# Four graph layers in one kernel: moves between partitions taken from DMA to TensorE, layer 1 nested, tables issued by ScalarE, other buffers and plan constants

## The chip, the cores and the metric

One core of a Trainium2 chip runs the whole program. The metric is the device time of one execution in microseconds (us); the time before is the median of nine runs. The engines are named as in the profile: PE (matmul), PEld (its weight loads), DVE (VectorE), ACT (ScalarE), POOL (GpSimd), SP (SyncE, which here only issues DMAs).

## The reference

Sixteen graphs of 1024 nodes with 64 features each pass four layers. `adj` is a 0/1 matrix with about four neighbours per node. Each layer normalizes its input, applies relu and adds its result to `x`:

```python
# layer 0: one normalized hop (adjacency plus self), one weight, relu
h = relu(layernorm(x)); x = x + relu(norm_adj @ (h @ L0_kernel))
# layer 1: h and its three hops side by side, one weight over all four
g = (adj + I) * d[:, None] * d[None, :]          # d = 1 / (sqrt(row sum) + 1e-7)
outs = [h, g @ h, g @ g @ h, g @ g @ g @ h]
x = x + concat(outs) @ L1_W.T + L1_b
# layer 2: for each node, sort its neighbours' features (self included, some removed
# when there are more than ten), weighted sum of three quantiles, then a small MLP
agg = 0.25*q(0.25) + 0.5*q(0.5) + 0.25*q(0.75)
x = x + (relu((h + agg) @ W1 + b1) @ W2 + b2) * nodemask
# layer 3: one plain hop
x = x + adj @ (h @ L3_weight) + L3_bias
```

## The kernel before

**Per graph.** `fast` runs over the graphs `b`; `first(b)` notes the stages graph, rank, lists, table and layer1, and `second(b)` the stages sort and out. All instructions are first noted by a planner and later issued.

- graph (`fast_graph`): eight row tiles of 128x1024 are loaded by SP into five `row` buffers. ACT counts neighbours (`junk_row`), PE transposes the row, ACT copies it into `at` (fp8), DVE finds up to eight neighbours per node (`found`).
- rank (`by_degree`): nodes are sorted by their number of neighbours, so that the sort later needs few slots for most; `near` holds the neighbour numbers in that order.
- lists (`dilated`): removals, weights, and the indices for the gathers: `idx`, `self_idx` and `shared_idx`.
- table and layer1 (`fast_to_table`): layers 0 and 1. A hop is `fast_product`: `u` is split into three bf16 parts, and each part gives 16 matmuls against `at`; `add_turned` adds the self term, and ACT copies the sum out (`prod_sb`, features on partitions). The normalized result `h2` is then written to a table in DRAM, from which POOL gathers.
- sort (`fast_quantiles`): POOL gathers neighbours' rows from the table into the slots of `a`, DVE sorts the slots (`a` and `b` by turns), weighs and sums them.
- out (`unsorted`, `fast_to_output`): one-hot matrices `back` bring the result to node order, then the MLP and layer 3.

**Shared gathers.** Slot `k` of node tile `s` is full (128 rows) or only partly used. The partial slots, 13 pieces (`packed`), are packed into four gathers of up to 128 rows (`staged0` to `staged3`). A piece that begins at row `at` of its gather must begin at row 0 in `a`. So each piece is moved twice between partitions: its indices into `shared_idx` (line 1274, in the lists stage), and its gathered rows out of `staged` into `a` (line 1373, in the sort stage). Both are SBUF-to-SBUF DMAs issued by SP, 26 per graph. The unused rows of `a` are filled with a large number by ACT (`a<-big`).

**Layer 1.** After `h`, DVE makes `u` for the first hop. Aside from that PE transposes `h`, multiplies it with the first weight block, and the result with the bias is added to `x`. Each of three hops gives `prod_sb`, which goes through its weight block into the PSUM bank `acc` (`times`), and in the first two hops also through a transpose into the next `u`. The sum in `acc` is scaled and added to `x`.

**Order.** `Plan` decides the order of every engine's instructions ahead of time. `cost` gives each instruction a length and a landing time (a plain DMA: 0.1 us of its issuing queue). `order` gives each step a wanted time from its chain within the graph, `PERIOD` per graph and an offset `LATER` per stage, lists the steps engine by engine (`listed`), repeats that `PASSES` times and keeps the list with the shortest length by its own costs. On the chip each engine and SP take their lists strictly in order. Buffers, which the planner knows, limit how many graphs are under way: four `at`, five `x`, two `near`. PSUM's banks are named per phase by `bank`.

Of the kernel before, what the change touches and what calls it, by code (L numbers as in the profile page):

```python
# [11 lines left out]
F32 = mybir.dt.float32  # L12
# [4 lines left out]
U32 = mybir.dt.uint32  # L17
AF = mybir.ActivationFunctionType
ALU = mybir.AluOpType
# [22 lines left out]
    "_0": dict(u=1, prod_sb=1),  # L42
    "_1": dict(u=2, h=1, h2=2, prod_sb=2, ft_sb=1),
    "_b": dict(agg=1, ft_sb=1, hid=1, u=1, prod_sb=1),
}
ROW_BUFS = 5
PASSES = 3
PERIOD = 474.0

LATER = dict(  # L50
    graph=-2909.0, rank=-1697.0, lists=-2440.0, table=-1118.0, layer1=688.0, sort=610.0, out=2073.0
)
# [41 lines left out]
def over_features(v):  # L94

    return v.unsqueeze(2).to_broadcast([v.shape[0], v.shape[1], F])
# [265 lines left out]
def cost(engine, op, out, ins, kw):  # L362
# [8 lines left out]
    if op == "dma_start":  # L371
        return 0.1, 2.2 if n < N else 3.6
    if engine == "tensor":
# [35 lines left out]
class Kernel:  # L409
# [7 lines left out]
    def constants(self, pool, work, psum):  # L417
# [60 lines left out]
        self.bias_parts = {}  # L478
        for name in ("L1_gnn_b", "L2_gnn_b2", "L3_gnn_bias"):
# [42 lines left out]
    def sorted_constants(self, pool, work, psum):  # L522
# [30 lines left out]
        self.before = pool.tile([w, w], BF16, name="before")  # L553
        nc.vector.tensor_scalar(self.before, kv[0:w, :], kvt, None, ALU.is_lt)

        node = self.counted(work, work, "node_of", [HT, 2], [[P, HT], [HT * P, 2]], step=1)
# [471 lines left out]
    def fast_pools(self, ctx):  # L1028
        def pool(what, bufs, space=None):
            made = self.pool(ctx, f"fast_{what}", bufs, space)  # L1030
            return Phased(self, PlanPool(self.plan, made, bufs, space is PSUM))

        self.plan = Plan(self.nc)
        self.p_at = pool("at", 4)
        self.p_small = pool("small", 2)
# [45 lines left out]
    def by_degree(self, b, n1, found):  # L1081
# [71 lines left out]

        near = self.p_lists.tile([P, T + 1, E], F32, name="near")
        nc.scalar.copy(near[:, 0, :], ps[:, 0, 0:E])
# [5 lines left out]
    def dilated(self, b, near, meta):  # L1161
# [107 lines left out]
        nc.vector.tensor_copy(idx, near)  # L1269
        shared = packed()  # L1270
        shared_idx = self.p_lists.tile([P, len(shared)], U32, name="shared_idx")
        for g, group in enumerate(shared):
            for s, k, at, r in group:
# [32 lines left out]
        nc.vector.tensor_tensor(flat, flat, part[:, 2], ALU.add)  # L1306
        return idx, shared_idx, self_idx, weights

# [14 lines left out]
    def fast_quantiles(self, table, lists):  # L1323

        nc = self.nc
        idx, shared_idx, self_idx, weights = lists
        agg = self.activations("agg")
        shared = packed()
        staged = []
        for g, group in enumerate(shared):  # L1330
            t = self.p_lists.tile([P, F], F32, name=f"staged{g}", bufs=1)
            r = sum(x[3] for x in group)
            self.gather(t[0:r, :], table, shared_idx[0:r, g : g + 1])
            staged.append(t)
        for lo, hi, n, halves in WIDTHS:

            alone = halves > 0
            count = hi - lo + halves - alone
            a = self.p_sort.tile([P, count * n * F], F32, name=f"a{n}", bufs=2)
            b = self.p_sort.tile([P, count * n * F], F32, name=f"b{n}", bufs=1)  # L1340
            av = a.rearrange("p (g k f) -> p g k f", g=count, f=F)

            def place(s, k):
                return (k // n, k % n) if s == 0 else (s - lo + halves - alone, k)

            for s in range(lo, hi):
                rows = rows_of(s)
                cap = len(rows)

                empty = [k for k, r in enumerate(rows) if r < P]  # L1350
                empty += range(cap + 1, n * (2 if halves and s == 0 else 1))
                while empty:
                    group, k = place(s, empty[0])
                    many = 1
                    while many < len(empty) and place(s, empty[many]) == (group, k + many):
                        many += 1
                    nc.scalar.copy(
                        av[:, group, k : k + many, :],
                        self.big.unsqueeze(1).to_broadcast([P, many, F]),
                    )  # L1360
                    empty = empty[many:]
                own = self.own(idx, s)
                group, k = place(s, cap)
                self.gather(av[:, group, k, :], table, self_idx[:, s : s + 1])
                for k, r in enumerate(rows):
                    if r == P:
                        group, i = place(s, k)
                        self.gather(av[:, group, i, :], table, own[:, k : k + 1])
            for t, members in zip(staged, shared):
                for s, k, at, r in members:  # L1370
                    if lo <= s < hi:
                        group, i = place(s, k)
                        nc.sync.dma_start(out=av[0:r, group, i, :], in_=t[at : at + r, :])
            r = self.sorted_slots(a, n, F, b)
# [41 lines left out]

    def fast_product(self, at, u, plus_self):

        nc = self.nc
        ps = self.bank("prod", (P, HT * P))  # L1420
        for n, part in enumerate(self.parts(u)):
# [223 lines left out]
    def fast_to_table(self, b, at, rs, table):  # L1645

        nc = self.nc
        x = self.p_x.tile([P, T, F], F32, name="x", bufs=5)
        for half in range(2):
# [22 lines left out]
        self.times(ps, pt, 0)  # L1672
        y = self.p_x.tile([P, T, F], F32, name="y", bufs=1)
        self.by_node(y, ps, AF.Relu, d0)
# [4 lines left out]
        self.phase, self.plan.stage = "_1", "layer1"  # L1679
        norm, = self.fast_normed(0, x, None)  # L1680
        h = self.activations("h")
        self.by_node(h, x, AF.Relu, *norm)
        u = self.factor("u")
        nc.vector.tensor_tensor(u, h, over_features(d1), ALU.mult)
        ps = self.bank("node", (P, HT * P))
        for q in range(HT):
            pair = h[:, 2 * q : 2 * q + 2, :].rearrange("p h f -> p (h f)")
            nc.tensor.transpose(ps[:, q * P : (q + 1) * P], pair, self.ident)
        ht = self.factor("ft_sb").rearrange("p s f -> p (s f)")
        nc.scalar.copy(ht, ps)  # L1690
        ps = self.bank("node")
        self.biased(ps, "L1_gnn_b")
        self.times(ps, ht, 1, start=False, one_group=True)
        nc.vector.tensor_tensor(x, x, ps, ALU.add)
        acc = self.bank("acc")
        for k in range(1, 4):
            pt = self.fast_product(at, u, True)
            self.times(acc, pt, 1 + k, start=k == 1, stop=k == 3, one_group=True)
            if k < 3:
                ps = self.bank("node")  # L1700
                for q in range(HT):
                    nc.tensor.transpose(
                        ps[:, 2 * q : 2 * q + 2, :], pt[:, q * P : (q + 1) * P], self.ident
                    )
                u = self.factor("u")
                self.by_node(u, ps, AF.Copy, d11)
        y = self.p_x.tile([P, T, F], F32, name="y", bufs=1)
        self.by_node(y, acc, AF.Copy, d1)
        nc.vector.tensor_tensor(x, x, y, ALU.add)
# [5 lines left out]
        for half in range(2):  # L1715
            nc.sync.dma_start(
                out=nodes(table[0:N, :].rearrange("(o n) f -> o n f", o=1), half),
                in_=h[:, half::2, :],
            )
        return x, h  # L1720

    def fast_to_output(self, b, at, x, ot):
# [4 lines left out]
        for half in range(2):  # L1727
# [4 lines left out]
            for q in range(HT):  # L1732
# [6 lines left out]
                )  # L1739
        y = self.p_x.tile([P, T, F], F32, name="y", bufs=1)  # L1740
        mask = self.mask[:, b * T : (b + 1) * T]
# [99 lines left out]
```

## Time and profile before

| | |
|---|---|
| nine runs | 1745.21 to 1766.52 us, median 1755.19 us |
| profiled execution | 1746.21 us |
| its span, first to last instruction | 1744.3 us |
| granted TensorE clock, mean | 0.798 |
| busy: DVE, PE, POOL, ACT | 1150.4, 1113.9, 964.1, 838.9 us |
| HBM read and written | 103.05 MB and 8.39 MB |

The profiled execution is one run; durations of instructions come from it. Busy times count an engine's own work; time in which it waits for a semaphore or only issues a DMA is not busy. All instructions of the planner carry the line of its issuing loop (L351), so they are told apart by what they write and read: `a<-staged` is the move of gathered rows into `a`, `shared_idx<-idx` that of the indices, `table<-h` the write of a table. An fp32 matmul stands in the trace as two records. The chain of work that ended last is followed back from the last instruction; `SPq` in it is time in which SP's queue issued DMAs, and "another core or an unknown queue" is waiting whose releaser the profile can't name.

### The profile page before, as it was taken

The page shows a single profiled execution, that of the slowest core. Times are in us where ns is not written, and L with a number is a line of the kernel's source. Part 1 is how long each engine was busy: PE and PEld are TensorE (multiplying, and loading weights), DVE is VectorE, ACT ScalarE, POOL GpSimd, SP SyncE. Part 2 cuts the span into 40 slices and gives each one's busy share as a digit, 9 for nine tenths or more (in the row PEclk, how much of TensorE's full clock was granted, in tenths as well). Part 3 has the DMA queues.
Part 4 walks back from the last instruction along what each step waited for, and adds up shares of the span by engine and source line. Part 5 has one row for each costly group of instructions (what it writes and reads, how often), then busy time and mean ns, then how long its engine had stood idle before and what let it go on. Part 6 is the DMA issues. An engine that isn't in the chain of part 4 may idle for free.

```text
span 1744.3 us, 24520 instructions
## 1 busy us (share of the span) xinstructions
PE 1113.9 (64%) x7784; PEld 625.9 (36%) x7784; DVE 1150.4 (66%) x2929; ACT 838.9 (48%) x2307; POOL 964.1 (55%) x767
## 2 busy tenths in 40 slices
PE   2664496778586675867478685847468665583345
PEld 1342253344253342434244353423234342341122
DVE  6953275588786684948478695847668476676381
ACT  4864352475555472645266565535365453433021
POOL 0006327487668284736728484855838467586700
PEclk9886697788888896888689797968779678696657
DMA  5433101132313141221323222221213121111100
GB/s 162 144 109 98 51 16 47 33 105 64 107 46 103 38 123 53 56 75 48 104 52 105 58 79 68 91 53 44 79 47 108 44 65 33 25 33 31 29 8 9
DMA packets 117624, 115.20 MB, mean 66 GB/s; under 512 B 87692, under 2 KB 88044, under 8 KB 117484
## 3 DMA queue, kind: packets, MB, share of 16 engines
q1 hardware_dynamic: 91756, 82.08, 15.5%
q0 software_dynamic: 25344, 31.38, 8.0%
q8 instruction: 64, 1.05, 0.2%
q14 instruction: 76, 0.62, 0.1%
q10 hardware_dynamic: 384, 0.07, 0.0%
HBM read 103.05 MB, written 8.39 MB: 64 GB/s over the span
## 4 chain that ended last, share of the span: by engine, by line
DVE 28%; issue 17%; another core or an unknown queue 15%; PE 13%; ACT 9%; SPq 7%; DMA 6%; POOL 4%; DVEq 0%; POOLq 0%; ACTq 0%
PE prod L351 10%; DVE b L351 7%; SPq L351 7%; DVE a L351 5%; POOL a L351 4%; DVE found L351 3%; DMA row<-in_adj_dram 2%; PE node L351 2%; ACT junk_row L351 1%; DVE stats L351 1%; ACT u L351 1%; DVE x L351 1%; DVE rest L351 1%; ACT y L351 1%
## 5 line engine op out<-in xcount | busy, mean ns | idle before, releaser
L351 POOL DMA_INDIRECT a<-table,idx x512 | 661.4, 1292 | 162.0 <-issue 155.3
L351 POOL DMA_INDIRECT a<-table,self_idx x128 | 166.9, 1304 | 236.1 <-DMA table<-h 76.7
L351 PE MATMUL prod<-at,u 128*64 128x512 fp8e4 x1280 | 207.9, 446 | 68.9 <-ACT u L351 36.5
L351 DVE TENSOR_TENSOR b<-a 128x768 f32<-128x768 f32 (+4 forms) x224 | 177.8, 824 | 88.6 <-DMA a<-staged 65.1
L351 PE MATMUL prod<-at,rest 128*64 128x512 fp8e4 x1280 | 188.1, 421 | 33.1 <-DVE rest L351 16.8
L351 DVE TENSOR_TENSOR a<-b 128x1536 f32<-128x1536 f32 (+4 forms) x192 | 199.1, 1070 | 4.4 <-ACT b L351 3.3
L351 PE MATMUL prod<-at,lo 128*64 128x512 fp8e4 x1280 | 177.1, 396 | 30.6 <-issue 25.6
L351 ACT CAST at<-tr 128x1024 fp8e4<-128x1024 bf16 x128 | 127.6, 1022 | 142.2 <-remote 107.0
L351 ACT ACTIVATE junk_row<-row,unit 128x1024 bf16<-128x1024 f32 x128 | 148.0, 1156 | 67.6 <-DMA row<-in_adj_dram 65.8
L351 DVE TENSOR_SCALAR back<-numbers,meta 128x1024 bf16<-128x1024 f16 x128 | 61.3, 488 | 157.4 <-remote 91.7
L351 DVE FIND_INDEX8 found<-ones,row 128x8 uint32<-128x1032 f32 x128 | 156.4, 1225 | 0.0
L351 POOL DMA_INDIRECT staged<-table,shared_idx x64 | 81.4, 1272 | 131.1 <-DMA table<-h 62.0
L351 PE MATMUL tr<-ident_bf,row 128*128 128x128 bf16 x1024 | 90.5, 235 | 97.1 <-ACT at L351 68.4
L351 PEld LDWEIGHTS <-u 128*64 128x64 bf16 x1280 | 77.5, 123 | 186.5 <-issue 70.4
L351 PEld LDWEIGHTS <-lo 128*64 128x64 bf16 x1536 | 94.6, 115 | 137.6 <-issue 63.2
L351 PEld LDWEIGHTS <-rest 128*64 128x64 bf16 x1536 | 93.4, 120 | 132.6 <-issue 50.4
L351 ACT COPY prod_sb<-prod 128x512 f32<-128x512 f32 x80 | 46.9, 587 | 171.8 <-PE prod L351 120.1
L351 ACT ACTIVATE h<-x,norm_bias,rstd 128x64 f32<-128x64 f32 x256 | 90.1, 434 | 60.7 <-DVE norm_bias L351 46.5
L351 PEld LDWEIGHTS <-row 128*128 128x128 bf16 x1024 | 70.9, 106 | 122.8 <-issue 118.0
L351 PE MATMUL prod<-back,agg 128*64 128x512 bf16 x256 | 66.6, 458 | 70.0 <-DVE back L351 30.0
L351 PE MATMUL prod<-ident,u 128*128 128x128 f32 x512 | 87.3, 311 | 24.5 <-issue 24.3
L351 ACT COPY b<-a 128x768 f32<-128x768 f32 (+2 forms) x128 | 69.0, 588 | 60.0 <-DVE a L351 46.9
(209 smaller groups left out, 1983.3 us busy)
## 6 DMA issues: line engine op xcount, KB each, us to landing
row<-in_adj_dram SPq DMA_DIRECT2D x128, 512.0 KB
a<-table,idx POOLq DMA_INDIRECT x512
x<-in_x_dram SPq DMA_DIRECT2D x32, 128.0 KB
table<-h SPq DMA_DIRECT2D x32, 128.0 KB
out_dram<-x SPq DMA_DIRECT2D x32, 128.0 KB
a<-table,self_idx POOLq DMA_INDIRECT x128
staged<-table,shared_idx POOLq DMA_INDIRECT x64
a<-staged SPq DMA_DIRECT2D x32, 20.0 KB
```

The source lines that it names most:

```text
L351: f(*[real(x) for x in s.args], **{k: real(x) for k, x in s.kw.items()})
```

## The change

- The two moves of each piece become matmuls with a shifted matrix of ones (`shift`, built once). The index move reads `near` (fp32) instead of `idx` and is made in the sort stage; its 13 one-column products of a graph go to the PSUM bank `moved`, and ACT copies them to `shared_idx`. Each piece of `staged` is a product of 64 columns into `moved` (eight pieces to a bank), which ACT copies into `a`. The fills of `a` come first for all slots.
- Layer 1 is written as a nested sum: the last block's product first, then for each of three hops `d11` times the sum, a hop, and the next block added inside `fast_product` by one 512-column product (`more`). The bank `acc` is gone; each hop ends in four transposes. `h` of layer 1 is not made, `u` is made at once with the root of the degree in its factor, and the bias is added on DVE.
- The tables are written from ACT's queue instead of SP's.
- `y` uses `u`'s buffers; `at` has five buffers, `x` six, `near` three, `ft_sb` of layer 1 two.
- `cost` gives a plain DMA 0.35 or 0.5 us instead of 0.1; `PERIOD` and `LATER` have other values.

```diff
-    "_1": dict(u=2, h=1, h2=2, prod_sb=2, ft_sb=1),
+    "_1": dict(u=2, h2=2, prod_sb=2, ft_sb=2),
...
-PERIOD = 474.0
+PERIOD = 566.0
-    graph=-2909.0, rank=-1697.0, lists=-2440.0, table=-1118.0, layer1=688.0, sort=610.0, out=2073.0
+    graph=-1558.0, rank=-1340.0, lists=-1357.0, table=-796.0, layer1=-156.0, sort=321.0, out=1580.0
...
     if op == "dma_start":
-        return 0.1, 2.2 if n < N else 3.6
+        return 0.35 if n == N else 0.5, 2.2 if n < N else 3.6
...
+        d = self.counted(work, work, "col_past", [3 * P], [[1, 3 * P]], base=-P, step=-1)
+        self.shift = pool.tile([P, 3 * P], F32, name="shift")
+        nc.vector.tensor_scalar(self.shift, d, 0.0, None, ALU.is_equal)
...
-        self.p_at = pool("at", 4)
+        self.p_at = pool("at", 5)
...
-        near = self.p_lists.tile([P, T + 1, E], F32, name="near")
+        near = self.p_lists.tile([P, T + 1, E], F32, name="near", bufs=3)
...
-                nc.sync.dma_start(
-                    out=shared_idx[at : at + r, g : g + 1], in_=self.own(idx, s)[0:r, k : k + 1]
-                )
...
+        ps = self.bank("moved")
+        for g, group in enumerate(shared):
+            for n, (s, k, at, r) in enumerate(group):
+                nc.tensor.matmul(
+                    ps[:, 0, g : g + 1],
+                    lhsT=self.shift[0:r, P - at : 2 * P - at],
+                    rhs=self.own(near, s)[0:r, k : k + 1],
+                    start=n == 0,
+                    stop=n == len(group) - 1,
+                )
+        shared_idx = self.p_lists.tile([P, len(shared)], U32, name="shared_idx")
+        nc.scalar.copy(shared_idx, ps[:, 0, 0 : len(shared)])
+        pieces = [(g, *x) for g, group in enumerate(shared) for x in group]
+        staged = {}
+        for first in range(0, len(pieces), T):
+            ps = self.bank("moved")
+            some = pieces[first : first + T]
+            for n, (g, s, k, at, r) in enumerate(some):
+                rows = sum(x[3] for x in shared[g])
+                if g not in staged:
+                    staged[g] = self.p_lists.tile([P, F], F32, name=f"staged{g}", bufs=1)
+                    self.gather(staged[g][0:rows, :], table, shared_idx[0:rows, g : g + 1])
+                nc.tensor.matmul(
+                    ps[0:r, n, :],
+                    lhsT=self.shift[0:rows, P + at : P + at + r],
+                    rhs=staged[g][0:rows, :],
+                    start=True,
+                    stop=True,
+                )
+            for n, (g, s, k, at, r) in enumerate(some):
+                av, group, i = places[s, k]
+                nc.scalar.copy(av[0:r, group, i, :], ps[0:r, n, :])
...
-            for t, members in zip(staged, shared):
-                for s, k, at, r in members:
-                    if lo <= s < hi:
-                        group, i = place(s, k)
-                        nc.sync.dma_start(out=av[0:r, group, i, :], in_=t[at : at + r, :])
...
+            if more and n == 0:
+                nc.tensor.matmul(ps, lhsT=more[0], rhs=more[1], start=False, stop=False)
...
-        x = self.p_x.tile([P, T, F], F32, name="x", bufs=5)
+        x = self.p_x.tile([P, T, F], F32, name="x", bufs=6)
...
-        norm, = self.fast_normed(0, x, None)
-        h = self.activations("h")
-        self.by_node(h, x, AF.Relu, *norm)
+        norm, = self.fast_normed(0, x, root)
         u = self.factor("u")
-        nc.vector.tensor_tensor(u, h, over_features(d1), ALU.mult)
+        self.by_node(u, x, AF.Relu, *norm)
...
         ps = self.bank("node")
-        self.biased(ps, "L1_gnn_b")
-        self.times(ps, ht, 1, start=False, one_group=True)
-        nc.vector.tensor_tensor(x, x, ps, ALU.add)
-        acc = self.bank("acc")
-        for k in range(1, 4):
-            pt = self.fast_product(at, u, True)
-            self.times(acc, pt, 1 + k, start=k == 1, stop=k == 3, one_group=True)
...
+        self.times(ps, gt, 4)
+        for k in range(3, 0, -1):
+            u = self.factor("u")
+            self.by_node(u, ps, AF.Copy, d11)
+            pt = self.fast_product(at, u, True, (self.wbd[:, k, :], gt))
+            ps = self.bank("node")
+            for q in range(HT):
+                nc.tensor.transpose(
+                    ps[:, 2 * q : 2 * q + 2, :], pt[:, q * P : (q + 1) * P], self.ident
+                )
+        y = self.factor("u")
+        self.by_node(y, ps, AF.Copy, d1)
+        nc.vector.tensor_tensor(x, x, over_tiles(self.bias["L1_gnn_b"]), ALU.add)
         nc.vector.tensor_tensor(x, x, y, ALU.add)
...
-            nc.sync.dma_start(
+            nc.scalar.dma_start(
                 out=nodes(table[0:N, :].rearrange("(o n) f -> o n f", o=1), half),
```

More of the change, by code (lines that the diff above doesn't have):

```diff
@@ L478, in constants @@
         self.bias_parts = {}
-        for name in ("L1_gnn_b", "L2_gnn_b2", "L3_gnn_bias"):
+        for name in ("L2_gnn_b2", "L3_gnn_bias"):
             rest = work.tile([1, F], F32, name="bias_rest")
@@ L1269, in dilated @@
         nc.vector.tensor_copy(idx, near)
[L1270 to L1273, printed above, removed]
-                nc.sync.dma_start(
-                    out=shared_idx[at : at + r, g : g + 1], in_=self.own(idx, s)[0:r, k : k + 1]
-                )
         self_idx = self.p_lists.tile([P, T], U32, name="self_idx")
@@ L1306, in dilated @@
         nc.vector.tensor_tensor(flat, flat, part[:, 2], ALU.add)
-        return idx, shared_idx, self_idx, weights
+        return idx, near, self_idx, weights
     def own(self, idx, s):
@@ L1325, in fast_quantiles @@
         nc = self.nc
-        idx, shared_idx, self_idx, weights = lists
+        idx, near, self_idx, weights = lists
         agg = self.activations("agg")
         shared = packed()
[L1329 to L1334, printed above, removed]
+        sorts, places = [], {}
         for lo, hi, n, halves in WIDTHS:
@@ L1339, in fast_quantiles @@
             a = self.p_sort.tile([P, count * n * F], F32, name=f"a{n}", bufs=2)
+            sorts.append((lo, hi, n, halves, alone, count, a))
+            av = a.rearrange("p (g k f) -> p g k f", g=count, f=F)
+            for s in range(lo, hi):
+                for k in range(n * (halves if halves and s == 0 else 1)):
+                    group = k // n if s == 0 else s - lo + halves - alone
+                    places[s, k] = av, group, k % n
+        for s in range(T):
+            rows = rows_of(s)
+            empty = [k for k, r in enumerate(rows) if r < P]
+            empty += [k for q, k in places if q == s and k > len(rows)]
+            while empty:
+                av, group, k = places[s, empty[0]]
+                many = 1
+                while many < len(empty) and places[s, empty[many]][1:] == (group, k + many):
+                    many += 1
+                nc.scalar.copy(
+                    av[:, group, k : k + many, :],
+                    self.big.unsqueeze(1).to_broadcast([P, many, F]),
+                )
+                empty = empty[many:]
@@ L1340, in fast_quantiles @@
+        for lo, hi, n, halves, alone, count, a in sorts:
             b = self.p_sort.tile([P, count * n * F], F32, name=f"b{n}", bufs=1)
-            av = a.rearrange("p (g k f) -> p g k f", g=count, f=F)
-            def place(s, k):
-                return (k // n, k % n) if s == 0 else (s - lo + halves - alone, k)
             for s in range(lo, hi):
                 rows = rows_of(s)
[L1348 to L1364, printed above, removed]
@@ L1365, in fast_quantiles @@
+                av, group, i = places[s, len(rows)]
+                self.gather(av[:, group, i, :], table, self_idx[:, s : s + 1])
                 for k, r in enumerate(rows):
                     if r == P:
-                        group, i = place(s, k)
-                        self.gather(av[:, group, i, :], table, own[:, k : k + 1])
-            for t, members in zip(staged, shared):
-                for s, k, at, r in members:
-                    if lo <= s < hi:
-                        group, i = place(s, k)
-                        nc.sync.dma_start(out=av[0:r, group, i, :], in_=t[at : at + r, :])
+                        av, group, i = places[s, k]
+                        self.gather(av[:, group, i, :], table, self.own(idx, s)[:, k : k + 1])
@@ L1415, in parts, with fast_product @@
         yield lo
-    def fast_product(self, at, u, plus_self):
+    def fast_product(self, at, u, plus_self, more=None):
         nc = self.nc
@@ L1672, in fast_to_table @@
         self.times(ps, pt, 0)
-        y = self.p_x.tile([P, T, F], F32, name="y", bufs=1)
+        y = self.factor("u")
         self.by_node(y, ps, AF.Relu, d0)
@@ L1679, in fast_to_table @@
         self.phase, self.plan.stage = "_1", "layer1"
-        norm, = self.fast_normed(0, x, None)
-        h = self.activations("h")
-        self.by_node(h, x, AF.Relu, *norm)
+        norm, = self.fast_normed(0, x, root)
         u = self.factor("u")
-        nc.vector.tensor_tensor(u, h, over_features(d1), ALU.mult)
+        self.by_node(u, x, AF.Relu, *norm)
         ps = self.bank("node", (P, HT * P))
         for q in range(HT):
-            pair = h[:, 2 * q : 2 * q + 2, :].rearrange("p h f -> p (h f)")
+            pair = u[:, 2 * q : 2 * q + 2, :].rearrange("p h f -> p (h f)")
             nc.tensor.transpose(ps[:, q * P : (q + 1) * P], pair, self.ident)
-        ht = self.factor("ft_sb").rearrange("p s f -> p (s f)")
-        nc.scalar.copy(ht, ps)
+        gt = self.factor("ft_sb").rearrange("p s f -> p (s f)")
+        nc.scalar.copy(gt, ps)
         ps = self.bank("node")
-        self.biased(ps, "L1_gnn_b")
-        self.times(ps, ht, 1, start=False, one_group=True)
-        nc.vector.tensor_tensor(x, x, ps, ALU.add)
-        acc = self.bank("acc")
-        for k in range(1, 4):
-            pt = self.fast_product(at, u, True)
-            self.times(acc, pt, 1 + k, start=k == 1, stop=k == 3, one_group=True)
[L1699 to L1708, printed above, removed]
+        self.times(ps, gt, 4)
[7 more added lines that the diff above has]
+                    ps[:, 2 * q : 2 * q + 2, :], pt[:, q * P : (q + 1) * P], self.ident
+                )
+        y = self.factor("u")
+        self.by_node(y, ps, AF.Copy, d1)
+        nc.vector.tensor_tensor(x, x, over_tiles(self.bias["L1_gnn_b"]), ALU.add)
         nc.vector.tensor_tensor(x, x, y, ALU.add)
@@ L1739, in fast_to_output @@
                 )
-        y = self.p_x.tile([P, T, F], F32, name="y", bufs=1)
+        y = self.factor("u")
         mask = self.mask[:, b * T : (b + 1) * T]
```

## The prediction

> **What bounds the kernel now.** I read the busy row and the chain first, then the waits, then one stretch of the timeline.
>
> The page's busy row and chain rows:
>
> ```profile
> PE 1113.9 (64%) x7784; PEld 625.9 (36%) x7784; DVE 1150.4 (66%) x2929; ACT 838.9 (48%) x2307; POOL 964.1 (55%) x767
> ...
> DVE 28%; issue 17%; another core or an unknown queue 15%; PE 13%; ACT 9%; SPq 7%; DMA 6%; POOL 4%; DVEq 0%; POOLq 0%; ACTq 0%
> ```
>
> No engine is full. Per graph (a sixteenth) DVE does 71.9 us, PE 69.6, ACT 52.4, POOL 60.3. POOL's share is too low: the waits below show 624 gaps of about 0.3 us between gathers, so the gathers hold POOL for some (964.1 + 190.2)/16 = 72 us. The first and last table writes are issued at 134.7 and 1579.0 us, so a graph takes (1579.0 - 134.7)/15 = 96.3 us. Some 20 to 25 us per graph are thus waiting that no engine's load explains, and 7% of the chain, 122 us, is SP doing nothing but issue DMAs.
>
> The whole program's waits:
>
> ```profile
> POOL a L351 <- issue: 190.2, 624, 0.5
> POOL a L351 <- DMA table<-h: 76.7, 3, 32.4
> DVE b L351 <- DMA a<-staged: 65.1, 8, 13.5
> POOL staged L351 <- DMA table<-h: 62.0, 2, 49.7
> POOL staged L351 <- DMA a<-staged: 52.0, 6, 21.0
> ```
>
> POOL waits for tables, DVE's sort for the moved pieces, and the next graph's shared gathers for the same moves. All are transfers of SP's queue. The timeline around 780 us shows how they hang together (start, length, engine, in brackets the idle time before):
>
> ```profile
> 770.50 9.74 SPq L351 DMA_DIRECT2D shared_idx<-idx  x13
> ...
> 780.42 8.14 SPq L351 DMA_DIRECT2D a<-staged  x11
> 788.67 0.93 SPq L351 DMA_DIRECT2D table<-h  x2
> 789.70 0.97 SPq L351 DMA_DIRECT2D row<-in_adj_dram  x2
> 790.39 1.76 DVE L351 TENSOR_TENSOR b<-a 128x1536 f32<-128x1536 f32 x1 [11.92 <-DMA a<-staged]
> 790.77 1.20 SPq L351 DMA_DIRECT2D a<-staged  x2
> 792.00 1.02 POOL L351 DMA_INDIRECT a<-table,self_idx  x1 [28.48 <-DMA table<-h]
> ```
>
> Twenty-four tiny DMAs pass one after the other at 0.7 us each; a finished table and two row loads stand behind them; POOL idles 28.48 us and DVE 11.92. This stall I expect gone.
>
> **Part by part.**
>
> *Index and row moves off SP (gain).* Each graph has 13 pieces, each moved twice. The tile view gives the issue:
>
> ```profile
> L351 SPq DMA_DIRECT2D shared_idx<-idx x208: 3/654/1322, 86.5 to 1567.0; - x104
> ```
>
> 26 x 0.654 = 17.0 us of SP per graph, 272 us in all. SP's other issues: 128 rows x 0.328 = 42, tables 32 x 0.394 = 13, outputs 32 x 0.498 = 16, x loads 32 x 0.47 = 15, and `both` at the same price 15. Tables leave SP too, so (272 + 13)/373 = 76% of SP's 122 us on the chain go: **-93**. Bounds: -65 (only DVE's wait for the moves) to -272 (every issue was waited for).
>
> *Landings and row loads behind those issues (gain).* DMA holds 6% of the chain, 105 us, a third of that row loads. The moves' landings vanish and rows go out earlier; most others (gathers, `high`, the table itself) stay. Between 0 and -105; a third, **-35**, since row loads and moves are about that much of it.
>
> *The written-out order (gain).* `cost` prices a DMA issue at 0.1 us where the rows show 0.33 to 0.65, so the lists of all engines are made for an SP that is 14 us per graph too fast. The new prices, 0.35 and 0.5, stand near the rows and the 26 badly priced issues are gone. PERIOD and LATER are new as well, and one more `at` and `x` buffer could let a graph start earlier; but in the new DVE list the row scans of graph b+4 still stand behind the unsorting of graph b, as they do now. From +50 (a list can come out worse) to -150 (down to about 86 us per graph); I take **-30**, half of DVE's 65.1 us for the moved pieces, as the nearest row for waits put in the wrong place.
>
> *The same moves on PE (cost).* Nearest row for a 64-column fp32 product is `node<-w,hid` (42.0 us, two records per product, so 128 products: 0.33 us each). 13 x 0.33 = 4.3 us. The 13 one-column products are not in the trace: at least their two fp32 weight loads (37.7/128 = 0.29), at most 0.33; 0.30, as the weights dominate: 3.9.
>
> *Layer 1 nested (PE).* Gone: 12 products into `acc` (63.3/192 = 0.33 each, 4.0) and one bias product (13.6/32 = 0.4). New: three 128x128 by 512 fp32 products, like `prod<-ft_sb,w` (36.9/32 = 1.15 each, 3.5), and four transposes (22.0/128 = 0.17 each, 0.7). Net -0.2. PE: +8.0 us per graph, 128 in all. PE holds 13% of the span (227 us) on the chain for 1114 us of work, a fifth: **+26**; at most 128.
>
> A rule weighs on these 26 moves. The row charges 0.29 us of weight load for each. The Trainium skill ("TensorE: Matmul & The Clock Gate", LDWEIGHTS) says load time follows the number of columns over 1.2 GHz, 107 ns for 128, and puts a product of up to 64 columns at about 25 ns. By that the moves would cost 26 x 0.13 = 3.4 us per graph, an estimate, and the total would be some 15 us lower. The fp32 row disagrees by more than two, and I stay with it.
>
> *ACT (cost).* Eight more `u` activations (56.9/256 = 0.22: 1.8), 13 copies out of PSUM (like the 0.23 of `y<-node,mask`: 3.0), one small copy 0.2, and two table issues. ACT issues weights at the start in 0.39 to 0.69 us; 0.55 x 2 = 1.1. Sum 6.1 us per graph, 98 in all; ACT holds 9% of the chain (157 us) for 839 us of work: **+18**; at most 98. Behind a table issue in ACT's queue stand `at` and `prod_sb` copies, for which PE waits; the new list gives most table issues a wait on an earlier DMA's semaphore. If a landing were still under way there, a row load of 4 to 5 us would stop ACT.
>
> The skill's main page ("Trainium Kernel Development and Optimization", Key Constraints) says that DMAs from all queues share the same 16 engines, so that another issuer saves only issue time. That speaks against the table move: 0.8 us per graph on SP against 1.1 on ACT, a loss. In the trace the wait is not issue but SP's order, which the rule leaves out.
>
> *Layer 1's path.* Now `u` is one DVE product after `h` (0.68). Then: four transposes (17.7/64 = 0.28 each, 1.1), a copy 0.58, four products 1.3, eight activations 1.8: +4.1 us per graph, and up to 1.15 in each hop where the product isn't under DVE's splitting. At most 16 x 7 = 112 if graphs ran one by one; with four in flight a quarter counts, **+20** (28, less what the PE term holds). DVE: -0.68 for `u`, +0.32 for two 128x8 products: nothing.
>
> *Others at nothing:* `y` in the `u` buffer and the third `near` buffer (no instruction added); fills of `a` before the gathers (same copies, earlier, hidden by POOL's 72 us of gathers; uncovered, 45.4/16 = 2.8 us per graph). Bias added on DVE replaces an addition of the same length (0.68).
>
> Sum: 1744.3 - 93 - 35 - 30 + 26 + 18 + 20 = 1650 span. The profiled execution took 1746.21, 1.9 more than its span and 9.0 less than the median of 1755.19: about **1661** as a median. What is late next: POOL's gathers (72 us per graph) and PE (69.6 + 8.0 = 77.6).
>
> **Rivals.**
>
> *Deep gain.* Without SP the pace falls towards the busiest engine: PE's 77.6 us plus some 8 of waiting, 86. 15 x (96.3 - 86) = 155 less than 1755: 1600, and down to 1540. For it: no engine is over 75% loaded now. Against: 15% of the chain is waiting whose cause the profile doesn't name, and nothing in the change is seen to touch it.
>
> *SP was mostly covered.* Only DVE's 65 us come back, and the costs (26 + 18 + 20 = 64) eat them: 1755, spread over 1715 to 1765. For it: POOL is free to run other gathers while SP issues. Against: the 28.48 us.
>
> *Slower: PE waits for the gathers.* The 13 row products stand in PE's only queue, and in the new list each of the four shared gathers of a graph has its first product waiting on the gather's semaphore; all products behind wait too. `moved` is a single PSUM bank, so the second batch waits for ACT as well. Today only SP and DVE wait there. The chain shows 3.76 us from such a gather's start to its landing. 64 gathers x 3.76 = 241 on top of 1661, 1900, if PE always arrives early; at half, 1781. It decides from (1764 - 1661)/64 = 1.6 us per gather. Against: the list puts other products between gather and use.
>
> **How the numbers follow.** Forecast (1600 to 1715): 0.50. Deep gain (1540 to 1600): 0.15. SP covered (1715 to 1765): 0.17, of which 0.12 below 1746. PE waits (1764 to 1850): 0.18. About 0.5%, 9 us, is what can be told from no change. Faster 0.50 + 0.15 + 0.12 = 0.77, same 0.05, slower 0.18. The range, 1570 to 1775, leaves out about 0.05 below and 0.13 above.
>
> **What would show it.** Right: SPq near 2% on the chain, DVE's wait for `a<-staged` and POOL's for `table<-h` (139 us) mostly gone, PE busy near 1240, ACT near 935, tables about 90 us apart. Wrong: `moved` products with long idle time before them ended by `staged` (PE rival); ACT idle before `table`; or tables still 96 us apart with SP idle (covered).

## The result, and the profile after

The changed kernel takes **1871.79 us** as a median (20 runs, 1813.67 to 1957.51), the kernel before 1755.71 (62 runs): a ratio of **1.0464**, 95% interval 1.0395 to 1.0534. Ratios given with an interval compare the fast runs of each side, those within 1.5% of that kernel's fastest, so they differ from the ratios of the medians beside them (1.066 here). The changed kernel is thus slower by 4.6%; 1661 us, a ratio of 0.946, was forecast. The profiled execution, 1949.62 us, is a further run and lies near the top of the range of the twenty, so its lines are read for their kind more than for their size.

The page's busy row and chain row, and from its list of groups the two kinds of gathers (busy us, mean ns of one, then POOL's idle time before them):

```profile
PE 1296.0 (67%) x8376; PEld 712.1 (37%) x8376; DVE 1143.3 (59%) x2942; ACT 888.2 (46%) x2659; POOL 870.8 (45%) x768
...
PE 8%; DVE 4%; issue 3%; ACT 2%; DMA 1%; another core or an unknown queue 0%; DVEq 0%; ACTq 0%; POOLq 0%; SPq 0%
...
L351 POOL DMA_INDIRECT a<-table,idx x512 | 560.2, 1094 | 157.0 <-issue 156.7
L351 POOL DMA_INDIRECT staged<-table,shared_idx x64 | 106.4, 1662 | 637.0 <-DMA table<-h 410.0
```

DVE does the work it did before, in a span that is 203 us longer. The chain can be followed for only a fifth of the span, so it answers nothing here. The `a` gathers have become shorter, 1094 ns against 1292, and POOL idles before the shared ones. The waits of the whole program:

```profile
POOL staged L351 <- DMA table<-h: 410.0, 8, 58.3
POOL a L351 <- issue: 195.0, 637, 1.4
PE prod L351 <- issue: 183.0, 162, 5.7
ACT at L351 <- remote: 137.0, 19, 19.2
ACT ft_sb L351 <- remote: 134.7, 6, 40.2
```

DVE's wait for `a<-staged` is gone as forecast. POOL's wait for `table<-h`, which should have gone too, is three times what it was (62.0 + 76.7 before). ACT has long waits for a "remote" releaser on a program with one core, and PE waits 183 us for "issue", that is, for nothing the profile shows. A look at one of the 40 us waits: the busy times of the engines in two windows (the count of instructions in brackets), then the timelines of PE and ACT around the first of them.

```profile
core 0: us, PE busy (x) PEld busy (x) DVE busy (x) ACT busy (x) POOL busy (x), PEclk, DMA share, GB/s
1042.40:1079.90 37.50, 3.44 (x9) 0.60 (x5) 0.80 (x6) 0.34 (x2) 28.93 (x29) 0.54 0.21 57
1086.00:1098.00 12.00, 12.00 (x91) 7.93 (x90) 12.00 (x44) 11.22 (x33) 0.00 (x0) 0.97 0.14 44
```

```profile
1050.62 0.58 PE L351 MATMUL prod<-at,lo 128*64 128x512 fp8e4 x1 [0.84 <-issue]
1083.61 2.07 PE L351 MATMUL prod<-ft_sb,w 128*128 128x512 f32 x2 [32.41 <-ACT ft_sb L351]
...
1042.54 0.19 ACT L351 ACTIVATION_READ_ACCUMULATOR junk_row<-row,unit 128x1 f32 x1
1082.97 0.58 ACT L351 COPY ft_sb<-prod 128x512 f32<-128x512 f32 x1 [40.23 <-remote]
```

For 37.5 us POOL issues one gather after the other and nearly everything else stands. PE shows 9 products, with 91 in the 12 us after. PE is said to wait for ACT's copy, and the copy for "remote"; but what the copy reads is PE's own product, of which the last record starts at 1050.62. The step of the semaphore by which that product frees the copy is recorded at 1082.95, 32 us later. The copy starts at 1082.97, 3.1 us after the last of the gathers has ended (1079.85). This looks like gathers holding up PE, its signals included, and the experiments start from there.

### The profile page after: what moved, and what is told of

Read it like the earlier page. It is cut to its first block, busy times and chain, and to the rows that moved or that the text cites. A ratio compares the mean times of both kernels' runs of the same rounds, so it can differ in the third digit from the quotient of the medians.

```text
span 1947.7 us, 25345 instructions
## 1 busy us (share of the span) xinstructions
PE 1296.0 (67%) x8376; PEld 712.1 (37%) x8376; DVE 1143.3 (59%) x2942; ACT 888.2 (46%) x2659; POOL 870.8 (45%) x768
## 5 line engine op out<-in xcount | busy, mean ns | idle before, releaser
L351 POOL DMA_INDIRECT a<-table,idx x512 | 560.2, 1094 | 157.0 <-issue 156.7
L351 POOL DMA_INDIRECT staged<-table,shared_idx x64 | 106.4, 1662 | 637.0 <-DMA table<-h 410.0
L351 PE MATMUL prod<-at,lo 128*64 128x512 fp8e4 x1280 | 217.1, 408 | 100.7 <-issue 98.0
L351 DVE TENSOR_TENSOR a<-b 128x1536 f32<-128x1536 f32 (+3 forms) x192 | 200.6, 1071 | 14.9 <-ACT b L351 8.2
L351 DVE TENSOR_TENSOR b<-a 128x384 f32<-128x384 f32 (+4 forms) x224 | 179.3, 826 | 26.9 <-ACT a L351 20.8
L351 ACT ACTIVATE u<-node,d 128x64 f32<-128x64 f32 x640 | 139.8, 330 | 61.3 <-PE node L351 38.9
L351 POOL DMA_INDIRECT a<-table,self_idx x128 | 145.5, 1137 | 38.9 <-issue 38.3
L351 PE MATMUL tr<-ident_bf,row 128*128 128x128 bf16 x1024 | 103.1, 251 | 80.2 <-issue 41.6
L351 DVE TENSOR_TENSOR rest<-u 128x512 f32<-128x512 f32 x80 | 54.6, 684 | 106.7 <-ACT u L351 106.7
L351 PE MATMUL moved<-staged,shift 128*80 128x64 f32 (+11 forms) x416 | 55.5, 257 | 65.7 <-issue 33.2
```

Source lines behind the costliest of these rows:

```text
L351: f(*[real(x) for x in s.args], **{k: real(x) for k, x in s.kw.items()})
```

## The experiments

Six groups of kernels ran, each beside the kernel before on the same chip. **The chip turned out to have two conditions.** In three groups the kernel before took 1730 to 1754 us, as in the times above; in the other three 1488 to 1492. A condition lasted through a group. Of the four chips one was held in both of its groups, two were free in the only group that they had, and one was held in one group and free in another. They are called *held* and *free* here, for what the first experiment shows. Each ratio is against the kernel before of its own group.

**1. Gathers beside a stream of products, by itself.** A kernel that leaves the computation out: twelve phases parted by barriers, each with the same 288 products; with `phase()` alone, `phase(gathers=24)`, `phase(gathers=24, dve=20)`, `phase(dve=20)`, `phase(gathers=24, act=40)`, `phase(sp=24)`, `phase(sets=30)`, `phase(gathers=24, gap=64)`, `phase(gathers=24, gap=512)` and three on fp32.

> Twelve phases parted by barriers, the real computation left out: each runs the same stream of 288 fp8/bf16 matmuls on PE (phases 10 and 11: 64 fp32 matmuls; phase 12: none), alone (1, 10) or beside something else: 24 indirect gathers (2, 11), 24 gathers and 20 DVE tensor_tensor (3), the 20 DVE operations (4), 24 gathers and 40 ACT copies (5), 24 small DMAs from SP (6), 30 POOL memsets (7), 24 gathers with a memset of 64 or of 512 elements behind each (8, 9), 24 gathers without PE (12). Theory G (an unbroken run of gathers on POOL holds PE up while DVE is idle): phase 2 takes 20 us or more longer than phase 1, about the gathers' own 24 x 1.3 = 31 us; phase 3 no more than 5 us longer than phase 4; phases 6 and 7 within 2 us of phase 1; phase 11 is longer than phase 10 in the same way. Rival S (PE's late completions come from PE's own list, its waits for staged rows and the added fp32 matmuls, and gathers have no hold on PE): phases 1 to 9 all take PE the same time to within 3 us, and so do 10 and 11.

> The twelve phases again (the real computation left out). Theory C: where the kernel before takes near 1488 us, phases 1 and 2 both take PE 33 us as they did; where it takes near 1755 us, phase 2 (24 gathers, DVE idle) is 15 us or more longer than phase 1 without its start-up gap, and phase 3 (gathers beside a busy DVE) is not. Rival P (the hold, where there is one, comes from something the phases do not hold, such as row loads or table writes in flight): phases 1 and 2 equal to 3 us even where the kernel before takes 1755 us.

The first ran in a free group, the second in a held one. Windows of the free run, phase 2 up to the eighth gather and behind it:

```profile
92.80:103.40 10.60, 10.60 (x94) 5.30 (x92) 1.11 (x3) 0.00 (x0) 8.16 (x8) 0.92 0.15 21
103.40:124.00 20.60, 20.58 (x192) 10.35 (x188) 0.00 (x0) 0.00 (x0) 15.99 (x16) 1.00 0.23 27
```

The same windows of the held run (the second one split), then its phases 3 (busy DVE), 6 (small DMAs from SP) and 9 (a 512-element memset on POOL behind each gather):

```profile
92.60:103.20 10.60, 10.60 (x96) 5.42 (x93) 1.07 (x3) 0.00 (x0) 8.16 (x9) 0.95 0.14 21
103.20:110.50 7.30, 3.58 (x19) 1.01 (x17) 0.00 (x0) 0.00 (x0) 5.78 (x6) 1.00 0.24 29
110.50:123.70 13.20, 6.36 (x15) 1.26 (x14) 0.00 (x0) 0.00 (x0) 10.12 (x11) 0.51 0.23 25
...
153.80:185.00 31.20, 30.99 (x282) 15.97 (x278) 30.59 (x20) 0.00 (x0) 26.01 (x18) 0.98 0.15 18
316.00:345.00 29.00, 29.00 (x270) 14.72 (x266) 0.00 (x0) 0.00 (x0) 0.00 (x0) 1.00 0.09 19
457.00:487.00 30.00, 30.00 (x272) 15.36 (x270) 0.00 (x0) 0.00 (x0) 25.67 (x34) 0.97 0.16 20
```

Times of a stream go from its first product to DVE's read of the result. In the free run 24 gathers cost PE nothing: the stream takes 33.0 us. In the held run it takes 54.7. PE runs at full speed for eight gathers, 96 products in 10.6 us; then it makes 34 in 20.5 us, while 192 were made in the free run. The granted clock is still 1.00 in the first 7.3 us of this, so the clock is not the cause; its fall to 0.51 comes after. With DVE busy, with small DMAs, or with a pause of 0.54 us behind each gather there is no hold: 282, 270 and 272 products in windows of 29 to 31 us. ACT is not held (its 40 copies take 34.5 us in both), but does not help either: phase 5 takes 57.6 us. A memset of 64 elements leaves 55.0 us, and fp32 products are held alike (38.6 us against 17.2). The DMA share is the same in both conditions, and the packets of a gather all start within 2.7 us of its end in the held run, within 2.5 us in the free one: no backlog of transfers is seen.

One more thing differs in the traces. A gather steps semaphores when it lands, and each step leaves a record, 16 per gather. Counted in phase 2, all 384 are there in the free run and 108 in the held one, and they are missing from the start: 34 against 101 in the first 10.6 us, while PE still runs at full speed. So it is in the whole kernels: 15.7 to 15.9 records per gather in every free trace, 4.8 to 5.6 in the held ones without a pause. "Remote" goes with it: no free trace of a whole kernel has such a wait, each of these held ones has, so the names of releasers are less sure in held traces. Two readings stay open: that the gathers hold PE by their own work and signals, or that the recording of their landings does. Every run on record has a span and a clock from its own records, so none shows a time without recording.

**2. Is it the pace, or a busy DVE?** The same phases with other pauses.

> Ten phases with the same stream of 288 matmuls (the real computation left out): alone; 24 gathers back to back; 24 gathers with a POOL memset of 128, 256, 384 and 512 elements behind each; with a memset of 512 behind every second and every fourth; 24 gathers of 64 rows; 24 gathers beside 60 DVE operations that touch PSUM only. On a chip where gathers hold PE (the kernel before takes near 1755 us; on the other kind all phases take 33 us): theory Rate (PE is held where gathers follow each other faster than some pace): the stream's time falls step by step or at once from 55 us to 33 us between a memset of 64 (1.36 us apart, 55.0 us) and of 512 (1.79 us apart, 33.9 us), and the DVE operations in PSUM, which leave a gather at 1.0 us, do not help (50 us or more). Rival Port (it is a busy DVE or a memset's hold on a port that frees PE, not the pace): any memset from 128 up cures it, or the DVE operations in PSUM do.

This was a held group. Windows over the gathers of a phase: back to back; memset of 128, 256, 384 elements behind each; of 512 behind every second, then every fourth; gathers of 64 rows; beside DVE operations in PSUM (columns as above):

```profile
93.20:124.30 31.10, 19.72 (x117) 6.99 (x114) 1.07 (x3) 0.00 (x0) 24.08 (x24) 0.77 0.20 24
156.00:189.50 33.50, 26.33 (x152) 9.19 (x149) 1.12 (x3) 0.00 (x0) 29.10 (x47) 0.75 0.18 23
214.80:250.70 35.90, 34.52 (x274) 15.64 (x271) 1.11 (x3) 0.00 (x0) 31.57 (x47) 0.95 0.17 22
260.70:291.00 30.30, 30.30 (x276) 15.56 (x274) 1.07 (x3) 0.00 (x0) 26.92 (x38) 0.97 0.16 21
359.30:390.70 31.40, 31.40 (x281) 15.96 (x278) 1.08 (x3) 0.00 (x0) 26.40 (x32) 0.97 0.17 22
403.80:436.70 32.90, 24.14 (x152) 9.09 (x148) 1.04 (x3) 0.00 (x0) 26.58 (x29) 0.87 0.19 23
460.50:490.10 29.60, 15.90 (x87) 6.05 (x83) 1.11 (x3) 0.00 (x0) 22.55 (x24) 0.67 0.08 13
525.40:556.40 31.00, 16.58 (x90) 5.94 (x87) 29.46 (x44) 0.00 (x0) 23.94 (x24) 0.72 0.21 24
```

Put against the mean time from one gather's start to the next, the stream takes 56.3 us at 1.31, 52.2 at 1.41, 39.2 at 1.52, and 33.0 at 1.62. With a memset behind every fourth gather (1.39 on average) it is 50.1. With one behind every second (1.50) it is 37.8, but there the products themselves are done after 33.6 us, and only DVE's read of them is released late, 4.2 us after the last product:

```profile
388.91 2.25 PE L352 MATMUL prod<-at,lo 128*64 128x512 fp8e4 x16
395.33 0.69 DVE L352 TENSOR_TENSOR x<-x,prod 128x512 f32<-128x512 f32 x1 [34.89 <-remote]
```

DVE in PSUM, which leaves the gathers at 1.0 us, does not help, and half the rows do not either. So the hold goes with the pace. That a DVE which works in SBUF helps fits this: it slows a gather from 1.00 to 1.44 us, so that starts are 1.77 us apart. The landing records go with the pace as well: of 16 per gather 4.4 are there at 1.31 us, 6.1 at 1.41, 7.8 at 1.52, 12.0 at 1.62. What PE waits for, no line here names, and why it is so in one condition only isn't known.

**3. The changed kernel in both conditions.** Unaltered, three times.

> The changed kernel itself once more, unaltered, because the kernel before took 1488 us beside the first four experiments and not 1755, and because the twelve phases showed no hold of gathers on PE there. Theory C (the hold depends on the chip or its state; without it the change is worth what the forecast's sum said): where the kernel before takes near 1488 us, the ratio is 0.93 to 0.96; where it takes near 1755 us, 1.03 to 1.06. Rival R (the ratio belongs to the change, whatever the chip): 1.03 to 1.06 in both cases.

> The changed kernel, unaltered, on whichever kind of chip this is. Theory C: where the kernel before takes near 1488 us, 1385 to 1425 us (ratio 0.93 to 0.957; the two kernels closest to it gave 0.945 to 0.956); where it takes near 1750 us, 1.03 to 1.07 as before. Rival (moves on PE themselves cost, also without the hold): over 1440 us where before takes 1488.

> The changed kernel, unaltered, still wanted where gathers do not hold PE. Theory C: where the kernel before takes near 1488 us, 1385 to 1425 us (ratio 0.93 to 0.957). Rival (the moves on PE cost also without the hold): over 1440 us there. Where before takes near 1740 us: 1.03 to 1.07.

Held: 1845.58 us (four runs, 1780.19 to 1922.99) beside 1745.50, and 1802.25 beside 1730.20, a ratio of 1.0505 (1.0332 to 1.0678). Free: **1414.46 beside 1492.05, 0.9481 (0.9407 to 0.9554)**. The ratio belongs to the condition as much as to the change. The page and the waits of the free run:

```profile
PE 1154.3 (82%) x8376; PEld 669.5 (48%) x8376; DVE 1143.1 (81%) x2942; ACT 883.0 (63%) x2659; POOL 977.8 (69%) x768
...
L351 POOL DMA_INDIRECT a<-table,idx x512 | 661.7, 1292 | 156.8 <-issue 155.0
L351 POOL DMA_INDIRECT staged<-table,shared_idx x64 | 104.4, 1631 | 72.6 <-DMA table<-h 23.6
```

```profile
PEld moved L351 <- DMA staged<-table,shared_idx: 50.2, 31, 4.6
PE moved L351 <- DMA staged<-table,shared_idx: 39.8, 27, 4.3
```

The waits for tables are 23.6 us, not 410, and no "remote" is left among the large ones. Tables are issued from 123.5 to 1257.1 us, 75.6 apart.

**4. A pause in the kernel.** One thing is added to either kernel, at the place where planned instructions are issued, so that the order of all else stays (512 elements, or 256):

```diff
             f(*[real(x) for x in s.args], **{k: real(x) for k, x in s.kw.items()})
+            if s.f == "indirect_dma_start":
+                self.nc.gpsimd.memset(self.pause, 0.0)
```

> The changed kernel with one thing added: behind each indirect gather POOL clears 512 elements of a tile that nobody reads (0.54 us), the order of all else unchanged. Theory G (unbroken gathers hold PE, and that is why the change lost): on a chip where the kernel before takes near 1755 us, 1400 to 1560 us instead of 1846, although POOL gets 736 x 0.54 = 397 us more work; on a chip where it takes near 1488 us, slower than without by 0 to 80 us, 1400 to 1490. Rivals (the loss is in the change's own work): 1846 us or more, since nothing but work is added.

> The kernel before with the same memset of 512 behind each gather. Theory G: on a chip where the kernel before takes near 1755 us, 1480 to 1650 us; on one where it takes near 1488, 1488 to 1570. Rival (gathers hold PE only in the new order, the kernel before is free of it): slower than before on both, by 1 to 10%.

Held: the changed kernel takes 1620.59 us, 0.9349 of the kernel before (0.9260 to 0.9438); that with 405 us of work more on POOL. The forecast of 1400 to 1560 was too low, as POOL itself became the bound (chain row, and the pause's group):

```profile
POOL 77%; issue 8%; DVE 5%; PE 4%; DMA 2%; POOLq 1%; ACT 1%; SPq 1%; DVEq 0%; ACTq 0%
...
L353 POOL MEMSET pause<- 128x512 f32 x736 | 404.8, 550 | 0.5
```

The kernel before with the pause: 1692.23 us, 0.9766 (0.9689 to 0.9843), above the 1480 to 1650 expected, but below the kernel without it. So it was held as well, and the pause brings it less: it has fewer long runs of gathers (counted below).

> The changed kernel with a POOL memset of 256 instead of 512 elements behind each gather (0.33 instead of 0.54 us). With 512 POOL carried 77% of the chain of waits, so the 736 x 0.21 = 155 us that are saved should come off, less a rest of the hold (0.26 us for each gather 1.52 us apart, by the ten phases). Theory G: where the kernel before takes near 1750 us, 1480 to 1590 us; where it takes near 1488, 1390 to 1450. Rival (512 was needed, the hold returns with 256): 1620 us or more where the kernel before takes near 1750.

> The kernel before with the memset of 256 behind each gather. Theory G: where it takes near 1750 us without, 1570 to 1690 us; where near 1488, 1480 to 1540. Together with the run before it shows what the change is worth with the hold eased on both sides: 4 to 8% if the forecast's sum was right about the parts it had, nothing if not.

> The changed kernel with the pause of 256 elements, still wanted where the kernel before takes near 1740 us: at least the 1499 us that it took on the other kind of chip, at most the 1621 us of the pause of 512; theory G says 1500 to 1590 us, which would beat both kernels there by 9 to 14%. Rival (the hold returns with 256): 1620 us or more. Where before takes near 1488 us: 1499 us as it did.

Both groups were free, where there is no hold to lift, so these show the price alone: 1499.41 and 1502.96 us (1.0077 and 1.0072), and 1575.91 for the kernel before (1.0596). The shorter pause in the held condition was not seen. With the pause in both, the change is worth 1620.59/1692.23 = 0.958 held (512) and 1499.41/1575.91 = 0.951 free (256).

**5. Which part brings the hold?** First the planner's constants, exchanged between the kernels (`PERIOD`, `LATER`, the price of a DMA issue):

```diff
-PERIOD = 566.0
+PERIOD = 474.0
-        return 0.35 if n == N else 0.5, 2.2 if n < N else 3.6
+        return 0.1, 2.2 if n < N else 3.6
```

> The changed kernel with the planner's constants of before (PERIOD 474, the old LATER, 0.1 us for a DMA issue): moves on PE, nested layer 1, table writes on ACT and the buffers stay. Theory G (the written-out order makes the unbroken runs of gathers, and these hold PE up): 1690 to 1790 us, the time with gathers on and DVE idle falls from 483 us back towards 294. Rival S (the moves on PE and their waits for staged rows cost it): 1840 us or more. Rival L (the longer path of layer 1 and ACT's added work): 1800 to 1860.

> The changed kernel with the planner's constants of before once more, for the other kind of chip. Theory G with the order as the cause of longer runs of gathers: where the kernel before takes near 1755 us, 1690 to 1800 us (ratio under 1.02), with less time under held gathers than the changed kernel has. Rival O (the order has no part, any of the kernels that is faster on the fair chip meets the hold more often): 1800 us or more. Where before takes near 1488, 1418 us as it did.

> The kernel before with nothing changed but the planner's constants (PERIOD 566, the new LATER, 0.35 or 0.5 us for a DMA issue). Theory G: slower by itself, 1800 us or more, with more time in which gathers run and DVE is idle (over 380 us, against 294). Rivals S and L: within 2% of 1755 us, since the operations are the same.

> The kernel before with the new planner's constants alone, for a chip where the kernel before takes near 1750 us. If the order makes the runs: 1790 us or more. If it does not: 1700 to 1770 us. Where the kernel before takes near 1488 us: 1465 us as it did.

The changed kernel with the old constants: 0.9556 free (0.9500 to 0.9613) and 1.0475 held (1.0357 to 1.0593). In the held condition the order is thus not the cause; theory G was wrong on this. The kernel before with the new constants met the free condition twice: 0.9877 (0.9819 to 0.9936) and 0.9832 (0.9774 to 0.9889).

Then the moves: the changed kernel with `fast_quantiles` and the index moves of the kernel before, on SP. These are 13 moves of each kind per graph, not the 26 of the first expectation. The fills and the listing of the gathers come back with them, so that the three are not told apart.

```diff
-                nc.tensor.matmul(
-                    ps[0:r, n, :],
-                    lhsT=self.shift[0:rows, P + at : P + at + r],
-                    rhs=staged[g][0:rows, :],
...
+            for t, members in zip(staged, shared):
+                for s, k, at, r in members:
+                    if lo <= s < hi:
+                        group, i = place(s, k)
+                        nc.sync.dma_start(out=av[0:r, group, i, :], in_=t[at : at + r, :])
```

> The changed kernel with the shared rows moved by SP's small DMAs again (26 idx and 26 row moves per graph), the rest of the change kept, the planner's constants too. Theory G: the moves on PE are not the cause, so 1830 us or more, and 90 us above that if SP's moves still sit in the chain. Rival S: back under 1790 us.

> The changed kernel with SP's moves back, for a chip where the kernel before takes near 1750 us. Theory M (SP's moves and their waits kept DVE and POOL out of step, so that gathers ran beside a busy DVE; taking them out makes runs of gathers without DVE): under 1790 us. Rival N (the nested layer 1, the tables on ACT or the order make the runs): 1810 us or more. Where the kernel before takes near 1488 us: 1409 us as it did.

> The changed kernel with SP's moves back, still wanted for a chip where the kernel before takes near 1750 us. Theory M (taking SP's moves out makes the runs of gathers without DVE): under 1790 us. Rival N (nested layer 1, tables on ACT or the order make them): 1810 us or more. Where before takes near 1488 us: 1409 us as it did.

Free: 0.9451 (0.9397 to 0.9506) and 0.9485 (0.9415 to 0.9555), the same as with the moves on PE. Held: **1668.36 us where the changed kernel took 1802.25 in the same group**, 0.9668 of the kernel before (0.9304 to 1.0032). The runs of the two, 1647.50 to 1708.51 and 1796.36 to 1807.27, do not overlap. POOL's waits, first of the changed kernel, then with SP's moves, both in that group:

```profile
POOL staged L351 <- DMA table<-h: 309.2, 9, 65.2
```

```profile
POOL staged L351 <- DMA a<-staged: 100.2, 12, 42.0
```

SP's moves made POOL wait in the middle of its gathers, for a `staged` buffer to be read out, 12 times and 100.2 us. Without them the gathers of a graph run through. Counted in the traces, gathers that are the ninth or later of a run with starts less than 1.45 us apart are 164 with SP's moves and 217 without; 145 in the kernel before and 248 in the changed one. At 1.1 us of lost PE time for each (1.30 less the sixth or so that PE still does) the 53 between the first two would be 58 us, an estimate, against 134 measured. The count isn't the whole account: with the old constants it is 176 in the held group, at 1817 us.

A reading that fits, though no run shows it by itself, is that the hold feeds itself: when PE is held, DVE runs out of work; with DVE idle, gathers go from 1.44 to 1.00 us; and at that pace they hold PE. In the free group the same kernel has 32 such gathers.

**A better version.** With the pause of 512 elements the changed kernel beats both kernels in the held condition (0.9349), but in the free one even 256 elements cost more than the change brings. With SP's moves kept it is at 0.9451 and 0.9485 free and at 0.9668 held, there from one group and with an interval (0.9304 to 1.0032) that includes no gain: the safer choice for both.

## Why the prediction was wrong

- **The step that failed** is the first, *index and row moves off SP*, -93. The chain's 7% for SP was taken as time to win. In the held condition those waits were also pauses for POOL: taking them out cost 1802.25 - 1668.36 = 134 us. In the free condition they were worth nothing that shows beside intervals of some 1% (0.9481 with the moves on PE, 0.9451 and 0.9485 with them on SP). *Landings and row loads*, -35, was priced on what waits behind the same moves; no run takes it alone. The sum has no term for what the gathers, once nothing stops them, do to PE: it stood at nothing.
- **What the profile did say.** The chain row gave 15%, 262 us, to "another core or an unknown queue", on a program with one core. The prediction used it only against the deep gain and let it stand unchanged. The kernel before is 1755 - 1490 = 265 us faster in the free condition. That the two numbers agree so closely may be chance. But the row goes with the hold: in no free trace does it show anything, and in the held traces of the kernel before, of the old constants and of SP's moves it shows 15, 17 and 10%.
- **Order**, -30: 1.2 and 1.7% of 1488, 18 and 25 us, in the free condition, on the kernel before. In size right; held, nothing is seen of it.
- **PE's 26 moves**: 71.1 + 54.4 us for 416 products in the free run, 7.8 us per graph, against 8.2 forecast. The Trainium skill ("TensorE: Matmul & The Clock Gate", LDWEIGHTS, and Back-to-back issue gap for the 25 ns) had led to 3.4, an estimate; the fp32 rows were the better guide. **ACT**: busy time grew by 49 us (888.2 - 838.9), where the forecast's terms without the issues make 80; a copy out of PSUM advances ACT by 25.7/208 = 0.12 us, not 0.23.
- **Layer 1's path**, +20, and the tables on ACT: with SP's moves and the new constants on both sides, what is left (nested layer 1, tables, buffers) gives 0.9451/0.9877 = 0.957 and 0.9485/0.9832 = 0.965 in the free condition. A gain of some 4% stands where a small loss was forecast. The parts of it were not taken alone, so whether another issuing queue saves no more than issue time, as the Trainium skill ("Trainium Kernel Development and Optimization", Key Constraints) says, was neither shown nor refuted here.
- **The rival that PE waits for the staged gathers** gave the right side (1764 to 1850) for another reason. PE's waits for them are 39.8 us in the free run, 0.6 per gather, with 1.6 as its turning point.
- **The sum** of 0.946 meets the free condition's 0.948, but with other terms, so the agreement is luck: the gain came for the most part from what was priced as cost, and of what was priced as gain only the order shows.

## What to carry to other kernels

Time that a chain gives to a releaser that cannot exist is a finding, not a remainder: look up what every engine does in those windows before a sum is made. A wait that is taken out may have been a brake on something else; ask at what pace the freed engine will run, and beside whom. And run the kernel before in each group: here the same two kernels compare as 1.05 and as 0.95.

## What was not expected of the hardware

- In one condition of the chip, more than some eight indirect gathers 1.30 us apart bring PE from 9 products per us to 1.7, and hold fp32 products too; 1.62 us apart there is no effect.
- The Trainium skill ("SBUF — State Buffer", Who interferes with whom) says: "PE and ACT never wait on anyone." ACT's 34.5 us in both conditions agree. PE's 54.7 against 33.0 do not, though these runs do not show that SBUF is the place.
- The hold goes by the number of gathers, not of rows: 64 rows instead of 128 hold PE as much (58.3 us at 1.24 us apart, against 56.3 at 1.31).
- The same program differs by 15% (1488 and 1755 us) between conditions that lasted through a group of runs, and one chip showed both.
- In the held condition part of the gathers' landing records is missing from the trace (4.4 of 16 per gather at 1.31 us apart, all 16 in the free one), and PE's semaphore steps can come long after its products (32 us in the changed kernel). Whether that is the hold's cause or a sign of it is open.
